# Logits through five banks in turn, and products with W in four 32-column tiles

## The chip, the cores and the metric

The kernel runs on one core of one Trainium2 chip. The metric is the time of one execution in device microseconds; the median of three runs before the change is 3207.64 us (3204.0 to 3208.25). The profile shows one further execution. Its engines are called PE (TensorE, the matrix array; PEld is its weight load), DVE (VectorE), ACT (ScalarE), POOL (GpSimd) and SP (SyncE, which issues most DMAs). PSUM, where TensorE writes its results, has eight banks of 128 partitions by 512 fp32 numbers; the kernel uses all eight.

## The reference

Sixteen graphs ("batches") of 1024 nodes with 256 features pass two layers. `adj` is 0 or 1. All arithmetic is fp32.

```python
x = _layernorm(x + L0_gnn(x, adj, ...))
x = _layernorm(x + L1_gnn(x, adj, ...))

# layer 0, 4 heads of 64
h = einsum('bnd,hde->bhne', x, W)
e_src = einsum('bhne,hte->bhtn', h, a_src); e_dst = einsum('bhne,hte->bhtn', h, a_dst)
weight = where(adj == 0, -1e9, leaky_relu(e_src[i] + e_dst[j], 0.01))
out = relu(softmax(weight) @ h + bias) + h
out = layer_norm_per_head(out) * ln_gamma + ln_beta

# layer 1, 8 heads of 32; queries, keys and values are the same normed rows
normed = layer_norm(x) * gamma1 + beta1
attn = softmax(where(adj > 0, q @ k.T / sqrt(32), -inf))
x = x + attn @ v
y = layer_norm(x) * gamma2 + beta2
out = x + gelu(y @ W1 + b1) @ W2 + b2          # 256 -> 1024 -> 256
```

## The kernel before

The kernel is one long program without loops on the chip. Two Python generators, `layer0` (line 1073) and `layer1` (1096), each yield after a small piece of work; a planner at the end of `fast_path` chooses whose piece comes next. Layer 0 works one batch ahead of layer 1, so that layer 0 of batch b+1 is laid between the pieces of layer 1 of batch b. The class `Pace` (92) keeps a running estimate of when each engine and each tile is free. It sets the order only: at run time each engine works through its own list in order, and waits where data or a buffer is not there yet. As all instructions are issued through one helper, the profile gives line 61 for all of them, and they are told apart by the names of their tiles.

Layer 0, per batch:

- `prepare` (528) takes the rows in four blocks of two times 128. Each block's x is transposed (`acc<-ident,xk`, copied to `xT` by ACT). For each of its two groups of 128 rows, two matmuls (halves c of the 256 features) multiply `xT` by `w0e` (W and the folded attention vectors, 264 columns) into one bank: `acc<-w0e,xT`, the "products with W". Between the two there is a yield, so the planner may put them into different gaps. ACT then takes four copies out of the bank (`apart`, `v`, `dinv`, `hb`), and DVE makes `z` and `v`. In the middle of each group `turn_mask` has ACT turn a loaded block of the adjacency into a byte mask (`mask<-ak`), and starts the load of the block three further on (a transposing DMA on SP's queue, three buffers). After each block the source terms are transposed (`acc<-ident,apart`) and pass through ACT (`rows`), memory (`esr`) and back (`cb`).
- `attention0` (646) has 32 steps, each of a pair of key blocks of one head. DVE makes the weights of a step (`p<-cb,dinv,mask`, two instructions), three steps ahead; TensorE multiplies them with `v` in 16 matmuls on 64-column tiles (`acc<-v,p`, 8 to a half step). A head's sums stay in one bank for its four steps, while the bank of the head before is read out.

Layer 1, per batch:

- `attention1` (804) has 32 steps. `exponentials` (822) computes four tiles of logits, 128 keys by 512 queries, as four concurrent matmuls on 32-row tiles (`ps<-nT`), and ACT takes each tile's exponential (`p<-ps`). One step later DVE multiplies with the mask (`p<-p,mask`, two a step). Three steps later (`LAG`) TensorE multiplies with the values on 32-column tiles: two heads with the exponentials moving (`po<-p,v` and `po<-p,unit`, four matmuls at once) and two with them held (`po<-v,p`, 32 matmuls of 33 columns). After every eighth step `heads_out` (904) copies the sums out (ACT `hs`, `oT`), transposes (`ident,oT`) and divides; `finish1` (931) normalises (ACT `o<-o,t,r`) and transposes.
- `mlp` (972) has matmuls on 64-column tiles, `ps<-yT,w_sb` with the GELU by ACT (`hid`), and `po<-w_sb,hid`.

The array of TensorE is thus used in four shapes: 32x128 (logits), 128x32 (attention 1's products), 64 columns (attention 0, MLP), and 128x128 (transposes, products with W).

PSUM is divided so: four banks `ps` in turn for the logits, the MLP's first stage and some transposes (ring `ps_s`); two banks `po`; and two single banks `acc0`, `acc1`, which `bank0` (395) hands out, the one taken longest ago first, unless it is `busy` with open sums. Layer 0 and, during attention 1, the transposes of layer 1 (`side_bank`, 408) use these two. Only in the last batch, when layer 0 has nothing left, do the logits take `acc0` and `acc1` too (`logits_tile`, 815).

The planner (1134 to 1178) counts progress: `WORK0` is layer 0's units per batch, `COURSE` says how far layer 0 should be at each point of layer 1, `SLACK` and `SLACK1` how far it may stray from that to fill a wait.

Of the kernel before, what the change touches and what calls it, by code (L numbers as in the profile page):

```python
# [31 lines left out]
F32 = mybir.dt.float32  # L32
# [7 lines left out]
P = 128  # L40
# [150 lines left out]
def fast_path(  # L191
# [24 lines left out]
    nc = Pace(tc.nc)  # L216
    B, N, D = x.shape
    H0, _, HO = w0.shape
# [176 lines left out]
    def bank0(shape, dtype=F32):  # L395
# [4 lines left out]
        return ps_a.tile(shape, dtype, f"acc{i}"), banks0[i]  # L400

    def bank0_ready():
        return min(ps_a.ready(f"acc{i}") for i in range(2) if not banks0[i]["busy"])
# [85 lines left out]
    def complete(chain):  # L489

        for item in list(chains):
            if item[0] is chain:
                while item in chains:
                    run(item)
# [33 lines left out]
    def prepare(b, hb, esr, cbs, v0, dinv, mask, first):  # L528
# [32 lines left out]
        for k in range(0, NB, GB):  # L561
# [13 lines left out]
            for g in range(GB):  # L575
# [6 lines left out]
                for c in range(DC):  # L582
                    nc.tensor.matmul(ph, xT[:, c, g * P : (g + 1) * P], w0e[:, c, :], start=c == 0, stop=c == DC - 1)
                    if c == 0:
                        if b:
                            turn_mask(k + g)
                        yield (0.45,)
                bank["busy"] = False
# [7 lines left out]
                if b == 0 and k == NB - GB:  # L596
                    first(g)
                yield 0.45, ready
                if g == 0 and b == 0:
# [204 lines left out]
    def attention1(half, values, mask, rinv, half_done, rest):  # L804
# [10 lines left out]
        def logits_tile():  # L815

            turn[0] = (turn[0] + 1) % 6
            if place[0][0] == B and turn[0] >= QUAD:
                return bank0([P, HALF])[0]
            return ps_s.tile([P, HALF], F32, name="ps")  # L820
# [46 lines left out]
        def logits_ready():  # L867
            return ps_s.ready("ps", QUAD)

        def outs_ready():  # L870
            return ps_o.ready("po", 2)

        for i in range(len(steps) + LAG):
            if i < len(steps):
                ready[i] = exponentials(*steps[i])
                advance()
# [256 lines left out]

    WORK0 = NB // GB * 2.0 + 2.0 + NB * H0 * 1.0
    REST1 = 3.5 * GB
    ATTN1 = REST1 + 2.0 + 2.5 * (NH * NB * H1 // QUAD)
    WORK1 = ATTN1 + NB // GB * (1.75 * FC / 2 + 3.5 * GB) - REST1
    SLACK = 0.083
    SLACK1 = 0.03
    STAY = 0.01  # L1140
    COURSE = [(0.0, 1.0), (REST1 + 1.0, 1.0), (ATTN1, 1.29), (WORK1 - 10.0, 2.0), (WORK1, 2.0)]

# [13 lines left out]
    while any(streams):  # L1156
# [5 lines left out]
        if all(streams):  # L1162
# [4 lines left out]
            if allowed and late[which] > max(late[other], 0.0) + 0.3:  # L1167
                which = other
        step = next(streams[which], None)
        if step is None:  # L1170
# [437 lines left out]
```

## Time and profile before

| | |
|---|---|
| median of three runs | 3207.64 us (3204.0 to 3208.25) |
| the profiled execution | 3203.7 us, span 3201.8 us |
| granted TensorE clock | 0.991 over the span |
| PE busy | 3148.4 us (98%), 67301 records |
| DVE busy | 2873.9 us (90%) |
| ACT busy | 1966.0 us (61%) |
| POOL busy | 497.8 us (16%) |
| DMA | 161.87 MB, 51 GB/s on the mean |

An fp32 matmul has two records here, since it is done in two passes with a weight load each; a transpose has one. A row of the timeline gives start, length, engine, line, operation, output <- inputs, the array's shape (rows*columns), the moving size and the count; what is in brackets is the engine's idle time before it and what ended it. A matmul's record is longer than the time between two starts, because matmuls are pipelined: intervals are read from start to start. Rows of windows give the stretch, its length, and then the busy time of PE, PEld, DVE, ACT and POOL, the granted clock, and the DMA's share and rate.

### The profile page before, as it was taken

What the parts mean: (1) busy time and instruction counts of PE and PEld (TensorE: products, weight loads), DVE (VectorE), ACT (ScalarE), POOL (GpSimd) and SP (SyncE); (2) the same over time, 40 slices, a digit from 0 to 9 for tenths busy, and PEclk for the clock granted to TensorE, in tenths of its full rate; (3) what the DMA queues carried; (4) which work ended last, traced back from release to release, by engine and by line L of the source; (5) the groups of instructions that cost most, each with busy time, mean ns of one, the idle gap of its engine ahead of it and who ended that gap; (6) DMA issues with size and microseconds to landing.
All of it is one profiled execution on the core that took longest, in us unless ns stands there. A gap on an engine that the chain in (4) does not pass through costs nothing.

```text
span 3201.8 us, 147006 instructions
## 1 busy us (share of the span) xinstructions
PE 3148.4 (98%) x67301; PEld 1966.1 (61%) x67301; DVE 2873.9 (90%) x4936; ACT 1966.0 (61%) x4258; POOL 497.8 (16%) x460
## 2 busy tenths in 40 slices
PE   6999999999999999999999999999999999999998
PEld 5557475565756657466575755757566575665745
DVE  6899998989989999899998989999899998999993
ACT  2664837648385673846748376483765838567383
POOL 1102011020211202112020110302112021120210
PEclk9799999999999999999999999999999999999999
DMA  7312203022130212203122031220302112010000
GB/s 156 78 26 65 53 26 88 20 68 49 32 85 23 71 40 58 65 20 77 31 71 53 26 85 23 68 50 26 91 17 75 43 46 75 20 48 20 28 10 16
DMA packets 208778, 161.87 MB, mean 51 GB/s; under 512 B 138322, under 2 KB 189522, under 8 KB 207188
## 3 DMA queue, kind: packets, MB, share of 16 engines
q1 hardware_dynamic: 200196, 115.66, 13.7%
q0 software_dynamic: 2592, 33.56, 5.3%
q8 instruction: 529, 8.67, 1.1%
q10 hardware_dynamic: 5360, 3.15, 0.4%
q14 instruction: 101, 0.83, 0.1%
HBM read 137.38 MB, written 48.50 MB: 58 GB/s over the span
## 4 chain that ended last, share of the span: by engine, by line
PE 96%; DVE 2%; issue 1%; DMA 1%; ACT 0%; POOL 0%; POOLq 0%; DVEq 0%; SPq 0%
PE po L61 39%; PE ps L61 33%; PE acc L61 24%; DVE p L61 1%; DVE hb L61 0%; DMA ak<-in_adj_dram 0%; DMA cb<-esr 0%; DMA esr<-rows 0%; ACT mask L61 0%; DVE relu L61 0%; DVE v0s L61 0%; DVE xl L61 0%; ACT sq L61 0%; ACT p L61 0%; ACT zz L61 0%
## 5 line engine op out<-in xcount | busy, mean ns | idle before, releaser
L61 DVE TENSOR_TENSOR p<-p,mask 128x1024 f32<-128x1024 f32 x1024 | 1186.3, 1217 | 1.3 <-ACT p L61 1.3
L61 ACT ACTIVATE p<-ps 128x512 f32<-128x512 f32 x2006 | 1041.9, 612 | 216.3 <-PE ps L61 201.3
L61 DVE SCALAR_TENSOR_TENSOR p<-cb,dinv,mask 128x512 f32<-128x512 f32 x1024 | 710.1, 744 | 8.6 <-DMA cb<-esr 8.4
L61 PE MATMUL ps<-nT 32*128 32x512 f32 x4012 | 627.4, 642 | 1.3 <-ACT p L61 1.3
L61 ACT ACTIVATE hid<-ps,b_sb 128x256 f32<-128x256 f32 x512 | 241.5, 472 | 610.9 <-PE ps L61 610.6
L61 PEld LDWEIGHTS acc<-v,p 128*64 128x64 f32 x16384 | 552.5, 140 | 77.8 <-DVE p L61 19.1
L61 PE MATMUL acc<-v,p 128*64 128x65 f32 x16384 | 575.6, 225 | 21.3 <-DVE p L61 16.8
L61 PEld LDWEIGHTS po<-v,p 128*32 128x32 f32 x32768 | 401.8, 109 | 316.5 <-issue 267.7
L61 PE MATMUL po<-p,v 128*32 128x512 f32 x2048 | 544.0, 606 | 0.0
L61 PE MATMUL po<-p,unit 128*32 128x512 f32 x2048 | 543.2, 606 | 0.0
L61 PE MATMUL ps<-yT,w_sb 128*64 128x256 f32 x4096 | 484.8, 380 | 0.0
L61 PE MATMUL po<-w_sb,hid 128*64 128x256 f32 x4096 | 481.4, 380 | 0.0
L61 PE MATMUL po<-v,p 128*32 128x33 f32 x32768 | 395.7, 198 | 8.5 <-issue 8.5
L61 POOL TENSOR_SCALAR r<-mv 128x4 f32<-128x4 f32 (+1 forms) x128 | 71.8, 561 | 2055.8 <-DVE mv L61 1852.4
L61 PEld LDWEIGHTS po<-w_sb,hid 128*64 128x64 f32 x4096 | 278.9, 137 | 141.9 <-issue 19.3
L61 PEld LDWEIGHTS ps<-yT,w_sb 128*64 128x64 f32 x4096 | 276.6, 137 | 124.5 <-issue 8.0
L61 POOL TENSOR_TENSOR r<-r,mhalf 128x8 f32<-128x8 f32 (+2 forms) x192 | 281.0, 1463 | 16.0
L61 PEld LDWEIGHTS po<-p,v 128*32 128x32 f32 x2048 | 78.2, 108 | 326.1 <-DVE p L61 153.2
L61 PEld LDWEIGHTS ps<-nT 32*128 32x128 f32 x4012 | 189.2, 183 | 128.7 <-ACT p L61 78.4
L61 PE MATMUL acc<-w0e,xT 128*128 128x264 f32 x480 | 167.0, 435 | 0.0
L61 POOL TENSOR_SCALAR r<-v0s 128x8 f32<-128x8 f32 x64 | 70.7, 1104 | 459.3 <-DVE v0s L61 458.1
L61 ACT ACTIVATE mask<-ak,shift_c 128x1024 uint8<-128x1024 bf16 x120 | 140.2, 1168 | 0.0
(121 smaller groups left out, 2454.3 us busy)
## 6 DMA issues: line engine op xcount, KB each, us to landing
cb<-esr SPq DMA_DIRECT2D x64, 512.0 KB
adjb<-in_adj_dram POOLq DMA_DIRECT2D x30, 1024.0 KB, 10.9
xk<-in_x_dram SPq DMA_DIRECT2D x64, 256.0 KB
xl<-in_x_dram SPq DMA_DIRECT2D x32, 512.0 KB
out_dram<-zz SPq DMA_DIRECT2D x64, 256.0 KB
ak<-adjb SPq DMA_TRANSPOSE x240
ak<-in_adj_dram POOLq DMA_DIRECT2D x8, 256.0 KB, 5.0
w_sb<-in_L_gnn_W_dram ACTq DMA_DIRECT2D x2, 1024.0 KB
```

The costliest lines, as they stand in the source:

```text
L61: return method(*args, **kwargs)
```

## The change

Three things change.

- The logits take five banks in turn: the four `ps` and a fifth. `lend` takes one of `acc0` and `acc1` from layer 0 when attention 1 of a batch begins, and `give_back` returns it after the last logits. While it is lent, layer 0 may go on to the point `PREP0` (the preparation and its first weights), and then the planner chooses layer 1 alone. The last batch, too, has five banks and not six.
- From the second batch on, a product with W is cut into four matmuls of 32 columns each. The yield between the two halves c is gone: a group of rows is one piece of eight matmuls.
- The planner's numbers follow: a group of rows counts 0.9 for its one piece, `WORK0` grows from 42 to 43, and `COURSE`, `SLACK` and `SLACK1` have other values.

```diff
@@ -399,6 +399,19 @@
         banks0[i].update(readers=[], taken=1 + max(bank["taken"] for bank in banks0))
         return ps_a.tile(shape, dtype, f"acc{i}"), banks0[i]
 
+    lent = []
+
+    def lend():
+        i = next(i for i in (1, 0) if not banks0[i]["busy"])
+        for chain in banks0[i]["readers"]:
+            complete(chain)
+        banks0[i].update(readers=[], busy=True)
+        lent.append(i)
+
+    def give_back():
+        i = lent.pop()
+        banks0[i].update(busy=False, taken=1 + max(bank["taken"] for bank in banks0))
+
     def bank0_ready():
         return min(ps_a.ready(f"acc{i}") for i in range(2) if not banks0[i]["busy"])
 
@@ -580,11 +593,17 @@
                 ph, bank = front_bank(b, [P, D + 2 * H0])
                 bank["busy"] = True
                 for c in range(DC):
-                    nc.tensor.matmul(ph, xT[:, c, g * P : (g + 1) * P], w0e[:, c, :], start=c == 0, stop=c == DC - 1)
-                    if c == 0:
-                        if b:
-                            turn_mask(k + g)
-                        yield (0.45,)
+                    for at in range(0, P, Q if b else P):
+                        m = Q if b else P
+                        nc.tensor.matmul(
+                            ph[at : at + m, :],
+                            xT[:, c, g * P + at : g * P + at + m],
+                            w0e[:, c, :],
+                            start=c == 0,
+                            stop=c == DC - 1,
+                        )
+                    if c == 0 and b:
+                        turn_mask(k + g)
                 bank["busy"] = False
                 nc.scalar.copy(apart[g][:, :, 0], ph[:, D + H0 : D + 2 * H0])
                 nc.scalar.activation(v0[:, k + g, :, HO], ph[:, D : D + H0], AF.Exp)
@@ -595,7 +614,7 @@
                 begin(scaling[-1], "vector", hb[-1])
                 if b == 0 and k == NB - GB:
                     first(g)
-                yield 0.45, ready
+                yield 0.9, ready
                 if g == 0 and b == 0:
                     turn_mask(k + 1)
                     yield 0.0, ready, xT
@@ -814,9 +833,9 @@
 
         def logits_tile():
 
-            turn[0] = (turn[0] + 1) % 6
-            if place[0][0] == B and turn[0] >= QUAD:
-                return bank0([P, HALF])[0]
+            turn[0] = (turn[0] + 1) % (QUAD + 1)
+            if turn[0] == QUAD:
+                return ps_a.tile([P, HALF], F32, f"acc{lent[0]}")
             return ps_s.tile([P, HALF], F32, name="ps")
 
         def exponentials(n, quad, jb):
@@ -865,12 +884,20 @@
         ready = {}
 
         def logits_ready():
-            return ps_s.ready("ps", QUAD)
+            free = [ps_s.ready("ps", i) for i in range(QUAD + 1)]
+            if not lent:
+                return free[QUAD]
+            wanted = [t % (QUAD + 1) for t in range(turn[0] + 1, turn[0] + 1 + QUAD)]
+            needs = ps_s.ready("ps", sum(t < QUAD for t in wanted))
+            return max(needs, ps_a.ready(f"acc{lent[0]}")) if QUAD in wanted else needs
 
         def outs_ready():
             return ps_o.ready("po", 2)
 
+        lend()
         for i in range(len(steps) + LAG):
+            if i == len(steps):
+                give_back()
             if i < len(steps):
                 ready[i] = exponentials(*steps[i])
                 advance()
@@ -1131,14 +1158,15 @@
 
 
 
-    WORK0 = NB // GB * 2.0 + 2.0 + NB * H0 * 1.0
+    WORK0 = NB // GB * 2.25 + 2.0 + NB * H0 * 1.0
+    PREP0 = NB // GB * 2.25 + 0.99
     REST1 = 3.5 * GB
     ATTN1 = REST1 + 2.0 + 2.5 * (NH * NB * H1 // QUAD)
     WORK1 = ATTN1 + NB // GB * (1.75 * FC / 2 + 3.5 * GB) - REST1
-    SLACK = 0.083
-    SLACK1 = 0.03
+    SLACK = 0.06
+    SLACK1 = 0.05
     STAY = 0.01
-    COURSE = [(0.0, 1.0), (REST1 + 1.0, 1.0), (ATTN1, 1.29), (WORK1 - 10.0, 2.0), (WORK1, 2.0)]
+    COURSE = [(0.0, 1.0), (REST1 + 0.0, 1.0), (ATTN1, 1.35), (WORK1 - 10.0, 2.0), (WORK1, 2.0)]
 
     def wanted():
         b, done = place[1]
@@ -1166,6 +1194,8 @@
             allowed = at0 < min(target + slack, place[1][0] + 2.05) if other == 0 else at0 > target - slack
             if allowed and late[which] > max(late[other], 0.0) + 0.3:
                 which = other
+            if lent and done0 >= PREP0:
+                which = 1
         step = next(streams[which], None)
         if step is None:
             streams[which], needs[which] = None, ()
```

## The prediction

> **What bounds the kernel now.** I read the page first: busy shares, then the chain that ended last.
>
> ```profile
> PE 3148.4 (98%) x67301; PEld 1966.1 (61%) x67301; DVE 2873.9 (90%) x4936; ACT 1966.0 (61%) x4258; POOL 497.8 (16%) x460
> ...
> PE 96%; DVE 2%; issue 1%; DMA 1%; ACT 0%; POOL 0%; POOLq 0%; DVEq 0%; SPq 0%
> ```
>
> TensorE is busy 98% and makes 96% of the chain, so only two things can move the end: the time TensorE needs for the same arithmetic, and the few waits it still has. The granted clock is full, so no clock term enters. Next, one batch split by stage (logits begin at 1087.5; the last two logits steps and the turn to the MLP lie in the second row; the MLP with layer 0's attention of the next batch in the third and fourth).
>
> ```profile
> 1087.00:1191.50 104.50, 104.50 (x2402) 53.29 (x2402) 93.72 (x141) 90.40 (x202) 9.73 (x10) 1.00 0.20 51
> 1191.50:1201.60 10.10, 10.10 (x353) 5.47 (x356) 10.10 (x11) 4.13 (x8) 0.00 (x0) 1.00 0.01 3
> 1201.60:1268.00 66.40, 66.40 (x1286) 52.60 (x1283) 63.23 (x132) 24.81 (x50) 18.64 (x17) 1.00 0.11 32
> 1268.00:1281.50 13.50, 13.50 (x188) 9.64 (x184) 12.09 (x27) 3.59 (x7) 3.15 (x3) 1.00 0.82 186
> ```
>
> The third number is PE, the fifth DVE, the sixth ACT. VectorE is close behind TensorE, and in the second row it has no idle time at all: the 98% hide a second bound. This batch takes 194.1 us (from its first logits at 1087.46 to the next batch's at 1281.59).
>
> Inside a stage I read TensorE's own timeline. Two stretches of attention 1, with and without a product with W (`w0e,xT`) between the products (`v,p`) and the next logits (`nT`):
>
> ```profile
> 1142.79 0.81 PE L61 MATMUL po<-v,p 128*32 128x33 f32 x64
> 1143.53 0.71 PE L61 MATMUL acc<-w0e,xT 128*128 128x264 f32 x2
> 1144.17 1.14 PE L61 MATMUL ps<-nT 32*128 32x512 f32 x8
> ...
> 1149.56 0.77 PE L61 MATMUL po<-v,p 128*32 128x33 f32 x64
> 1150.26 1.74 PE L61 MATMUL ps<-nT 32*128 32x512 f32 x8
> ```
>
> Start to start, products to logits takes 0.70 us without the W piece (1149.56 to 1150.26) and 1.38 with it (1142.79 to 1144.17): one piece costs 0.68. Its two passes of 264 columns need 0.22 each: the profile's passes of 512 columns start 0.45 apart (below), and 264/512 of that is 0.23. So about 0.2 us of every piece is the change of array shape, 128x32 to 128x128 to 32x128.
>
> The same stretch shows the only steady wait: logits take 1.14 undisturbed and 1.74 at 1150.26, because the fourth tile needs the last exponential of the step before. In this batch five logits steps are long (1.76, 1.74, 1.40, 1.65, 1.43): 2.3 us over 1.14 together. Adding up TensorE's start-to-start intervals over whole batches, I find some 190.5 us of pure work, 2.4 of such waits and 1 to 2 where products wait for a mask or weights from VectorE.
>
> **The change part by part.**
>
> *Products with W in column tiles.* By the two programs' orders of instructions, a batch has 16 single 128x128 products now: 13 stand alone between products and logits or transposes, three next to MLP work at the start. Afterwards there are 8 blocks of eight 32-column products; 6 stand directly behind the 128x32 products, without a change of shape, and 2 between logits and MLP. Their row is the nearest of the same shape:
>
> ```profile
> 1141.91 0.62 PE L61 MATMUL po<-p,v 128*32 128x512 f32 x1
> ...
> 1142.36 0.59 PE L61 MATMUL po<-p,v 128*32 128x512 f32 x1
> ```
>
> Four column tiles stream at once, and a pass of 512 takes 0.45. A block has four passes of 264: 4 x 0.225 = 0.90, plus some 0.02 at the change to logits that is there anyway: 0.92. Per batch, before: 13 x 0.65 (0.68 and, from the last product's start, 0.64) = 8.4, plus 1.6 for the other three; after: 6 x 0.92 + 2 x 1.0 = 7.5. Gain 2.5 us. Moves of other work nearly cancel: three of four transposes of source terms are parted from those of x (+0.15 each, a shape change more), and five half steps of layer 0's attention no longer stand between products and logits (-0.2 each); -0.4 to +0.5, taken as +0.1. Sum -2.4 a batch, 15 batches (the first batch's preparation keeps the full array): -36 us. It lies wholly on the path.
>
> A rule that speaks against it: the Trainium skill, "TensorEngine Tiling (Array Packing)", Performance Considerations, wants column tiles only where the stationary operand is at most 64 wide (here 128), and its Instruction Overhead puts about 60 cycles on each matmul. 720 more matmuls (960 for 240) at 60 cycles[...], 25 ns, would be 18 us as an estimate, so -18 instead of -36. The row of 64 records of 33 columns in 0.77 us (12 ns each at most, in four tiles) shows overheads of neighbouring tiles side by side, so I take -36 and keep -18 as an end.
>
> *The fifth bank.* Logits of a step then need only the third exponential of the step before, not the fourth. Exponentials follow each other 0.48 to 0.49 us apart (four in 2.06) and the first starts 1.16 after its logits (1147.61 to 1148.77). A bare step is 2.65 us (1147.61 to 1150.26). Fourth exponential: 1.16 + 2.06 + 0.05 = 3.27 after the logits' start, wanted at 2.67: the 0.60 above. Third: 2.78, so 0.11, and 0 in the step after one that waited. But bare steps become more: 84 of 512 logits follow products directly now, 237 after. I walked the 32 steps in ScalarE's new order with these intervals, a mask at 1.15, the four copies of a W block 0.4, head copies 0.75. W steps (2.65 + 0.92) hold exponentials, mask and copies (1.92 + 1.15 + 0.4 = 3.47) just within 3.57. What is left: the four `o` activations (2.08 in one row) now stand ahead of a bare step, 1.2 us; copies of heads 0.2; bare steps 0.7; and, with one bank fewer for everything else, the second W block of a batch waits about 0.45 for the copy of the first. Sum 2.7 against 2.4: +0.3. Ends: -1.2 (the long ones go too) and +2 (each late copy counts in full).
>
> *Layer 0 held back.* While a bank is lent, layer 0 stops at PREP0, so its attention runs wholly beside MLP. Queued behind VectorE there: 5 half steps' weights, 2.7 us of work, move from the first stage into the second; and TensorE has 56 MLP products instead of 40 behind the last step of layer 0, so weights must be done earlier.
>
> ```profile
> 1193.76 6.89 DVE L61 TENSOR_TENSOR p<-p,mask 128x1024 f32<-128x1024 f32 x6
> 1200.57 1.40 DVE L61 SCALAR_TENSOR_TENSOR p<-cb,dinv,mask 128x512 f32<-128x512 f32 x2
> 1202.72 0.20 DVE L61 RECIPROCAL ranges<-hs 128x8 f32<-128x8 f32 x1 [0.75 <-ACT hs L61]
> ```
>
> VectorE comes out of the masks about 6 us after the last logits begin; after the change I expect the same (6.3). The last weights are then 69.6 us of listed VectorE work later, 76 to 78.5 with 0 to 2.6 of its own idle time (now 2.5, of which the 0.75 above goes when VectorE arrives later); TensorE could use them at 75.6. Wait 0.4 to 3 us a batch, less 0.5 of now: I take +0.9.
>
> Course, slack and the new WORK0 cost no instruction; they only place the pieces, which is counted. DMAs are the same in number; masks' transposed loads stay three ahead, with two masks 3.5 us apart and then a pause, so nothing waits for them.
>
> Sum: -2.4 + 0.3 + 0.9 = -1.2 a batch, 15 batches -18; the last batch (five banks instead of six, no layer 0) 0 to +2. From the profiled execution's 3203.7 (span 3201.8, 1.9 around it) to 3186; the median of the runs lies 3.9 higher, 3207.6, and gives **3190**.
>
> **Rivals.**
> *Waits go with the bank.* If logits' waits fall to 1.2 and VectorE keeps up, only shapes and the bank count: -2.4 - 1.2 = -3.6 a batch, -54: 3154. For it: the fifth bank takes 0.5 of every long step. Against: three times as many bare steps.
>
> *VectorE becomes the bound (slower).* In the MLP stage, if it keeps its 2.5 us of idle and arrives 1.5 later, weights come 4.4 late instead of 0.5: +3.9 + 0.3 - 2.4 = +1.8 a batch, +27: 3235. It decides from 2.1 us more waiting than now. For it: 10.10 of 10.10 in the second row. Against: most of its idle is waiting for work that will be there.
>
> *One bank is too few for the side work (slower).* Some 23 W blocks and transposes a batch pass through it; from 0.1 us each the gain is gone, at 0.2 it is +2.2 a batch, +33: 3240. Against: most follow each other by a step of 2.65 and are copied out within 1 us.
>
> *The tiles gain half* (the rule above), with the same waits: -18 + 18: 3208, no change.
>
> **How the numbers follow.** The forecast 0.48, waits go 0.18, VectorE 0.15, one bank 0.07, half gain 0.12. About 0.2% (6.4 us) is what a measurement can tell from no change, 3201 to 3214. Range: from the first rival's 3154 to 3225, which leaves out the outer half of the slower cases. Faster: 0.18, nearly all of 0.48 and 0.03 of half gain: 0.67; same 0.12; slower 0.21. The likeliest case's own range is 3172 to 3204.
>
> **What would show it.** Right: a W group of 128x32 shape with passes 0.22 apart, held products to logits over a W block in 1.6 us; logits rows of 1.14 to 1.25 in most bare steps and one or two long ones beside the `o` activations; weights' waits (`acc` after `p`) up by about 1 us a batch; TensorE's batch near 193.2. Wrong: passes of W more than 0.3 apart, TensorE waiting for copies out of the single `acc` bank many times a batch, or gaps of several us before layer 0's products late in the MLP.

## The result, and the profile after

| | before | after |
|---|---|---|
| median of the runs shown with the result, us | 3207.9 (3204.0 to 3209.5) | 3170.3 (3166.4 to 3178.2) |
| profiled execution, its span, us | 3203.7, 3201.8 | 3170.4, 3168.6 |
| one batch, mean of the 2nd to the 15th, us | 194.9 | 192.8 |

The ratio is 0.9888 with a 95% interval of 0.9867 to 0.9909: the changed kernel is 1.1% faster. The sign was forecast rightly and the time lies in the range of 3154 to 3225 us, but the gain is 37.6 us where 17.6 were forecast, and the time lies just outside the likeliest case's own range (3172 to 3204). The size is what the experiments had to explain.

Two words are used below as in the prediction. A *W block* is the products with W of one group of 128 rows. A *bare step* is a step of layer 1's attention in which the logits follow the products directly, with no other work of TensorE between them.

The page of the changed kernel, its busy times and the shares of the chain that ended last:

```profile
PE 3114.9 (98%) x68741; PEld 1941.2 (61%) x68741; DVE 2877.3 (91%) x4936; ACT 1945.5 (61%) x4258; POOL 487.7 (15%) x460
...
PE 94%; ACT 3%; DVE 1%; DMA 1%; issue 1%; SPq 0%; POOL 0%; POOLq 0%; DVEq 0%
```

The list of groups, by shape, for the products with W, before and in tiles (after the bar busy us, mean ns of one, then idle time before them and what ended it):

```profile
L61 PE MATMUL acc<-w0e,xT 128*128 128x264 f32 x480 | 167.0, 435 | 0.0
...
L61 PE MATMUL acc<-w0e,xT 128*32 128x264 f32 x1920 | 132.1, 389 | 8.2 <-ACT hb L61 8.1 <-ACT rows L61 0.2
```

TensorE is still 98% busy, for 33.5 us less; VectorE is busy 3.4 us more and has the larger share. ScalarE, at 0% of the chain before, now makes 3% of it: the changed kernel has taken on waits for ScalarE. The W group shows one of them: it had no idle time ahead of it before, and now waits 8.1 us in all for `hb`, the last copy out of the one `acc` bank that is left.

One batch by stage, with the stretches of the prediction moved to this batch's first logits at 1074.6 and the last one ended at the next batch's (third number PE, fifth DVE, sixth ACT):

```profile
1074.15:1178.65 104.50, 104.02 (x2522) 51.15 (x2522) 94.65 (x144) 91.60 (x207) 10.14 (x9) 1.00 0.24 54
1178.65:1188.75 10.10, 9.88 (x381) 7.67 (x377) 10.10 (x13) 1.73 (x4) 0.00 (x0) 1.00 0.02 4
1188.75:1255.15 66.40, 66.40 (x1298) 52.67 (x1290) 65.54 (x138) 23.82 (x48) 15.53 (x15) 1.00 0.09 30
1255.15:1267.40 12.25, 12.25 (x117) 7.97 (x116) 9.51 (x18) 4.46 (x9) 4.58 (x5) 1.00 0.93 195
```

In the third row VectorE is busy 65.54 of 66.40 us, where it had 63.23 before. It has practically no idle time left from the end of layer 1's attention to the last weights of layer 0. The list of VectorE's waits in this part of the batch (us in all, times, longest) had three entries before the change and has none after it:

```profile
DVE hb L61 <- POOL r L61: 0.9, 1, 0.9
DVE ranges L61 <- ACT hs L61: 0.7, 1, 0.7
DVE zz L61 <- PE po L61: 0.7, 1, 0.7
```

The granted clock is still full, so the time is not a clock's.

TensorE's timeline over a W block shows the first step of the forecast as it was put: the products follow the W block's 16 records without a change of shape, and from products to logits it is 1.65 us (1109.04 to 1110.69; forecast 1.6).

```profile
1109.04 0.77 PE L61 MATMUL po<-v,p 128*32 128x33 f32 x64
1109.66 1.10 PE L61 MATMUL acc<-w0e,xT 128*32 128x264 f32 x16
1110.69 0.70 PE L61 MATMUL ps<-nT 32*128 32x512 f32 x3
```

The two waits that the forecast had named are there too, in the timeline of ScalarE and TensorE, at the second W block of the batch and beside the `o` activations:

```profile
1078.46 1.17 ACT L61 ACTIVATE mask<-ak,shift_c 128x1024 uint8<-128x1024 bf16 x1
...
1079.75 0.42 ACT L61 COPY hb<-acc 128x256 f32<-128x256 f32 x1
...
1080.23 1.10 PE L61 MATMUL acc<-w0e,xT 128*32 128x264 f32 x16 [0.48 <-ACT hb L61]
...
1153.11 2.08 ACT L61 ACTIVATE o<-o,t,r 128x256 f32<-128x256 f32 x4
...
1155.43 1.12 PE L61 MATMUL ps<-nT 32*128 32x512 f32 x3
...
1156.27 1.13 PE L61 MATMUL ps<-nT 32*128 32x512 f32 x2
```

The W block starts when the copy `hb` is done, which stands behind a mask of 1.17 us. The logits of 1155.43 need until 1157.76, when the transposes begin: 2.33 where undisturbed ones take 1.14, because four `o` activations of 2.08 us delayed the exponentials that free their banks.

VectorE's timeline at the end of layer 1's attention, where the forecast had it come late:

```profile
1175.91 8.03 DVE L61 TENSOR_TENSOR p<-p,mask 128x1024 f32<-128x1024 f32 x7
1183.86 5.38 DVE L61 SCALAR_TENSOR_TENSOR p<-cb,dinv,mask 128x512 f32<-128x512 f32 x8
...
1191.50 0.20 DVE L61 RECIPROCAL ranges<-hs 128x8 f32<-128x8 f32 x1
```

Masks end 6.8 us after the last logits begin (forecast 6.3). Then eight passes of layer 0's weights follow without a gap, and `ranges<-hs`, ahead of which VectorE stood idle for 0.75 us before the change, has no wait at all.

For the sum I took TensorE's start-to-start intervals over the 2nd to the 15th batch and set each against the median interval between the same two kinds of work in the profile before; what is over that is counted as waiting (the prediction's way, over 14 batches; rests under 0.1 are left out). In us per batch:

| | before | after | difference | forecast |
|---|---|---|---|---|
| work without waits, shape changes in it | 190.6 | 188.0 | -2.6 | -2.4 |
| logits waiting for a bank | 2.41 | 2.71 | +0.30 | with the next row +0.3 |
| W blocks waiting for their bank | 0 | 0.63 | +0.63 | |
| products waiting for masks | 1.02 | 0.44 | -0.58 | with the next row +0.9 |
| products of layer 0 waiting for weights | 0.70 | 0.87 | +0.17 | |
| all | 194.9 | 192.8 | -2.1 | -1.2 |

The last row is read directly from the timelines. How it is split over the rows above depends on the medians chosen, by up to some 0.5 us a row; sums of rows are firmer.

### The profile page after: what moved, and what is told of

Its sections match the earlier page's. It is cut to its first block, busy times and chain, and to the rows that moved or that the text cites. A ratio compares the mean times of both kernels' runs of the same rounds, so it can differ in the third digit from the quotient of the medians.

```text
span 3168.6 us, 150088 instructions
## 1 busy us (share of the span) xinstructions
PE 3114.9 (98%) x68741; PEld 1941.2 (61%) x68741; DVE 2877.3 (91%) x4936; ACT 1945.5 (61%) x4258; POOL 487.7 (15%) x460
## 4 chain that ended last, share of the span: by engine, by line
PE 94%; ACT 3%; DVE 1%; DMA 1%; issue 1%; SPq 0%; POOL 0%; POOLq 0%; DVEq 0%
PE po L61 39%; PE ps L61 29%; PE acc L61 26%; DVE p L61 1%; ACT p L61 1%; ACT mask L61 1%; ACT L61 1%; SPq L61 0%; DMA ak<-in_adj_dram 0%; DMA cb<-esr 0%; DMA adjb<-in_adj_dram 0%; DVE hb L61 0%; ACT hid L61 0%; POOL r L61 0%; ACT hb L61 0%
## 5 line engine op out<-in xcount | busy, mean ns | idle before, releaser
L61 ACT ACTIVATE p<-ps 128x512 f32<-128x512 f32 x1648 | 891.6, 617 | 152.9 <-PE ps L61 103.4
L61 PEld LDWEIGHTS acc<-v,p 128*64 128x64 f32 x16384 | 539.4, 140 | 70.8 <-DVE p L61 21.6
L61 PEld LDWEIGHTS po<-v,p 128*32 128x32 f32 x32768 | 393.6, 109 | 307.5 <-issue 264.7
L61 PE MATMUL acc<-v,p 128*64 128x65 f32 x16384 | 558.1, 225 | 23.4 <-DVE p L61 18.3
L61 PE MATMUL ps<-yT,w_sb 128*64 128x256 f32 x4096 | 477.9, 380 | 0.0
L61 PE MATMUL acc<-nT 32*128 32x512 f32 x800 | 449.1, 641 | 0.0
L61 POOL TENSOR_SCALAR r<-mv 128x4 f32<-128x4 f32 (+1 forms) x128 | 84.1, 657 | 2120.2 <-DVE mv L61 1861.6
L61 PE MATMUL po<-v,p 128*32 128x33 f32 x32768 | 385.9, 198 | 1.0 <-issue 1.0
L61 POOL TENSOR_TENSOR r<-r,mhalf 128x8 f32<-128x8 f32 (+2 forms) x192 | 302.0, 1573 | 16.0
L61 ACT ACTIVATE p<-acc 128x512 f32<-128x512 f32 x400 | 247.9, 620 | 45.8 <-PE ps L61 45.8
```

The source lines that it names most:

```text
L61: return method(*args, **kwargs)
```

## The experiments

All ratios are to the kernel before, run beside them; "a batch" is the mean of the 2nd to the 15th in the profiled run.

### Taking the change apart

**Full-array passes again (e2).** The changed kernel with

```diff
-                    for at in range(0, P, Q if b else P):
-                        m = Q if b else P
+                    for at in range(0, P, P):
+                        m = P
```

> The changed kernel with its W products as two full-array 128x128 passes again, in one piece; bank, hold and the order of everything else as in the changed kernel (237 bare steps). Theory (the tiles' gain is the change of shape of some 0.2 us at each of the standalone products, 120 x 0.17 = 20 us in the sum of TensorE's work): 3188 to 3192, and the profile shows products to logits over one piece in about 1.7 us against 1.6. Rival (four times as many matmuls cost their own overhead, so tiles are worth half or nothing): 3170 to 3180.

Measured 3184.0 us, 0.9937 (0.9924 to 0.9951); 13.7 us more than the changed kernel. Its timeline, TensorE over one block: from products to logits it is 1.76 us (1107.98 to 1109.74).

```profile
1107.98 0.75 PE L61 MATMUL po<-v,p 128*32 128x33 f32 x64
1108.66 1.16 PE L61 MATMUL acc<-w0e,xT 128*128 128x264 f32 x4
1109.74 0.70 PE L61 MATMUL ps<-nT 32*128 32x512 f32 x2
```

The two kernels have the same order of work, so their intervals can be set side by side: the W blocks cost 1.1 us a batch more with the full array, 16 us in all, of the theory's 20, and the whole batch is 0.9 us longer. The median lies between the two ranges: the tiles are worth some 14 us, over a third of the gain. The overhead of more matmuls is not seen; the rest of the gain does not need the tiles.

**Tiles and one piece alone (e1), full-array one piece alone (e3).** The kernel before with the edit below; e3 has `range(0, P, P)` and `m = P` in it.

```diff
-                    nc.tensor.matmul(ph, xT[:, c, g * P : (g + 1) * P], w0e[:, c, :], start=c == 0, stop=c == DC - 1)
-                    if c == 0:
-                        if b:
-                            turn_mask(k + g)
-                        yield (0.45,)
+                    for at in range(0, P, Q if b else P):
+                        m = Q if b else P
+                        nc.tensor.matmul(ph[at : at + m, :], ...)
+                    if c == 0 and b:
+                        turn_mask(k + g)
...
-                yield 0.45, ready
+                yield 0.9, ready
```

> The first part of the change alone: products with W in 32-column tiles and one piece, on the kernel before, with its four logits banks and layer 0 running on beside attention 1. Pure work of TensorE falls by 43 us by the shapes that are no longer changed, but the steps in which logits follow the products directly rise from 84 to 189, and with four banks each one behind a filled step waits about 0.6 us. Theory (the shapes pay only together with the fifth bank): most of the gain is eaten, 3180 to 3205 us, with logits rows of 1.7 us and over in most bare steps. Rival (the bank is worth little; the shapes alone make the gain): 3160 to 3170, as the whole change or better.

> The kernel before with its two half pieces of a W block joined to one, full-array passes, four banks, no hold. Joining saves 23 us of shape changes in TensorE's work and makes 189 bare steps of 84. Theory (with four banks a bare step costs about 0.6 us of waiting, which is more than a joined piece saves): no faster than before, 3205 to 3225. Rival (waiting is small): 3182 to 3190.

Measured 3355.6 (1.0466, 1.0452 to 1.0480) and 3381.2 (1.0548, 1.0534 to 1.0563). The sign is the theory's, the size is far beyond it. A batch of e1 is 10.8 us longer: logits wait 8.5 us instead of 2.4, which is the bank, and products of layer 0 wait 6.9 instead of 0.7, which nobody had forecast. The list of waits of e1 (us in all, times, longest) names the second:

```profile
PE acc L61 <- DVE relu L61: 82.0, 16, 5.3
```

and its timeline, VectorE and TensorE, shows it:

```profile
1457.29 1.22 DVE L61 TENSOR_TENSOR o<-o,x 128x1024 f32<-128x1024 f32 x1
1457.39 0.64 PE L61 MATMUL acc<-v,p 128*64 128x65 f32 x16
1458.55 1.41 DVE L61 BATCH_NORM_STATS2 st<-o 128x6 f32<-128x256 f32 x4
...
1462.80 0.42 DVE L61 SCALAR_TENSOR_TENSOR relu<-acc,ranges 128x256 f32<-128x256 f32 x1
...
1463.37 2.00 PE L61 MATMUL acc<-v,p 128*64 128x65 f32 x32 [5.34 <-DVE relu L61]
```

Joining the pieces made the kernel's planner place the first head of layer 0 so that the next one needs the same `acc` bank at once. The instruction that frees it, `relu`, is queued on VectorE behind the statistics of layer 1's output. TensorE waits 5.3 us for it, once a batch.

The clock adds to that. With each such wait TensorE's granted clock falls to half for 3.4 to 6.8 us, in each of the 14 batches from the 2nd to the 15th, while it stays full from the second batch on in the kernels before and after the change. The stretch behind the wait shown above (the clock is the third number from the end):

```profile
1463.40:1468.00 4.60, 4.60 (x45) 3.52 (x46) 3.09 (x6) 2.56 (x5) 0.00 (x0) 0.50 0.35 113
```

Outside the waits 4.2 us a batch run at half clock, so that some 2.1 us are lost (an estimate: half of them), in part inside the 6.9. e3 has the same waits and the same drops. So e1 measures the change's first part together with an order that the change avoids, not the first part alone.

**The bank taken back (e4).** The changed kernel with

```diff
-            turn[0] = (turn[0] + 1) % (QUAD + 1)
-            if turn[0] == QUAD:
-                return ps_a.tile([P, HALF], F32, f"acc{lent[0]}")
...
-        lend()
+        lent.append(0)
...
-                give_back()
+                lent.pop()
```

and `logits_ready` as before the change. `lent` now only holds layer 0 back.

> The changed kernel without the fifth bank: logits on four banks, both acc banks for the side work, layer 0 still held back for the length of layer 1, tiles as in the changed kernel. 297 bare steps. Theory (the bank takes about 0.5 us of waiting from each bare step): logits waits rise from 2.7 us to 6 to 8 us a batch, 3220 to 3250 us. Rival (layer 0's hold or VectorE, not the bank, is what counts): 3165 to 3185.

Measured 3240.8, 1.0112 (1.0096 to 1.0127): inside the theory's range. Logits wait 8.0 us a batch against 2.7. In its timeline a bare step behind a filled one is long:

```profile
1132.77 1.09 PE L61 MATMUL acc<-w0e,xT 128*32 128x264 f32 x15
1133.79 1.14 PE L61 MATMUL ps<-nT 32*128 32x512 f32 x8
1135.74 0.75 PE L61 MATMUL po<-v,p 128*32 128x33 f32 x64
1136.42 1.77 PE L61 MATMUL ps<-nT 32*128 32x512 f32 x8
```

The logits at 1136.42 take 1.77 (forecast for a bare step with four banks: 1.14 + 0.60). So the change without its bank is 70 us slower, twice the whole gain: tiles in one piece make bare steps, and bare steps need the bank. The order is not quite the same, since the planner counts with the banks: e4 has 297 bare steps and the changed kernel 237. The 70 us are the bank and these steps together.

**The hold alone (e11), and four banks without it (e10).** e11 is the kernel before with

```diff
+            if lent and done0 >= PREP0:
+                which = 1
```

where `lent` is filled at the start of layer 1's attention and emptied behind its last logits, and `PREP0 = NB // GB * 2.0 + 0.99`. e10 is e1 with the changed kernel's `WORK0`, `SLACK`, `SLACK1` and `COURSE`.

> The kernel before with layer 0 held back for the length of layer 1's attention and nothing else of the change: half pieces, four banks, the course of before. It shows the third step of the sum alone. Work of TensorE 3053.4 us (7 less), 174 bare steps of 84, which with four banks cost some 3 us a batch more. Theory A (as forecast: the work that moves to the second stage makes VectorE late, 0.9 us a batch more waiting for its weights and masks than before): waits for weights and masks of 2.5 to 3 us a batch, 3255 to 3265. Theory B (VectorE only gives up idle time; waits of products for masks and weights together do not grow): 1.0 to 1.6 us a batch, 3235 to 3250.

> The kernel before with products in tiles and one piece and with the changed kernel's numbers for course and slack, four logits banks, layer 0 not held. It differs from the kernel with four banks and layer 0 held by the hold alone (and the order that follows), and from the kernel with the first part alone by the course. Its work of TensorE is 3029.8 us, 159 bare steps. Theory (the 6.7 us a batch that products of layer 0 waited for weights in the kernel with the first part alone come from where the course puts the first products of layer 0 behind the last masks, not from the tiles): those waits fall to 0.3 to 1.5 us a batch, logits waits are 5 to 7, 3220 to 3240 us. Rival (without the hold VectorE comes late in any case): waits for weights of 4 us and more a batch, 3270 to 3330.

e11 measured 3229.3, 1.0070 (1.0053 to 1.0087), below both ranges and nearer to theory B. A batch is 1.6 us longer: work -0.5, logits +2.0. Waits for weights go from 0.70 to 1.41 and those for masks from 1.02 to 0.52: together +0.2 (with other medians -0.2) where the forecast had +0.9. This is the step on which theory A and the prediction stood. It costs next to nothing, because what the weights lose the masks get back.

e10 measured 3253.8, 1.0153 (1.0136 to 1.0170). Waits for weights are under 1 us a batch, so e1's 6.9 came from the course and slack, as its theory said. Its range was missed by 14 us because `relu` collides elsewhere: transposes wait 2.3 us a batch for it, and in 7 of the 14 batches the clock falls to half behind that wait (another 0.9 us a batch, estimated as for e1). e4 is 13 us faster than e10, but that is not the price of the hold alone, since e10 has this collision and 159 bare steps where e4 has 297.

### Is VectorE at its limit?

**Six passes added beside the MLP, to the changed kernel (e5) and to the kernel before (e15).**

```diff
+            if b and i in (12, 18):
+                for _ in range(3):
+                    nc.nc.vector.tensor_mul(spare, spare, spare)
```

in layer 0's attention, `spare` being 128x256 fp32.

> The changed kernel with six more VectorE passes over 128x256 elements of a spare tile in each batch from the second on (about 0.33 us each, 2.0 us together), three at each of two steps of layer 0's attention, where it runs beside the MLP; the order of all other work is the same. Theory A (VectorE has lost its idle time in this stage and sets when the last weights come, so every further us there is a us of TensorE's waiting): 1.5 to 2.0 us a batch, 3192 to 3200 us, and products waiting for weights (acc after p) up by as much. Theory B (VectorE is far enough from the bound that it takes 2 us without loss, so the waits forecast for it could not come): 3168 to 3176.

> The kernel before with the six VectorE passes over a spare tile beside the MLP in each batch that cost the changed kernel 29 us (2.5 us a batch by their measured 0.42 us each). Theory A (before the change VectorE's 2.5 to 4.5 us of idle time in that stage was real slack, which the hold then used up): part of the passes goes into the idle time, 0 to 1 us a batch, 3207 to 3222 us. Theory B (its idle time there was waiting for work that came late, so VectorE set the last weights before the change as well): 1.7 us a batch and more, 3230 to 3245 us.

One pass took 0.424 us, so 2.5 us a batch and 38 us in all. e5 measured 3199.7, 0.9976 (0.9966 to 0.9986): 29 us more than the changed kernel, 77% of what was added, and in theory A's range. e15 measured 3226.5, 1.0063 (1.0049 to 1.0077): 21 us, 56%, between A and B. The list of waits shows where it went, in the weight loads of layer 0's products (us in all, times, longest). The changed kernel:

```profile
PEld acc L61 <- DVE p L61: 21.6, 21, 3.5
```

and with the passes, e5:

```profile
PEld acc L61 <- DVE p L61: 33.5, 70, 3.0
```

The kernel before, and with the passes, e15:

```profile
PEld acc L61 <- DVE p L61: 19.1, 15, 3.3
...
PEld acc L61 <- DVE p L61: 41.5, 60, 2.9
```

By the intervals, waits for weights rise from 0.87 to 2.64 us a batch in e5, and little else moves. So VectorE sets the last weights after the change, and in part it did so before. Of the 2.5 us a batch, 1.1 disappeared in slack before the change and 0.6 after it: the change used up about half of the slack that was there, and ran over it by little.

**The same passes in layer 1's attention (e6)**, at `if i in (5, 10)` there.

> The same six VectorE passes over a spare tile (2.0 us a batch), but at two steps early in layer 1's attention, where VectorE has some 9 us of idle time a batch. Both theories: no change, 3168 to 3175 us; more would show that VectorE's whole time, not its place, counts.

Measured 3202.4, 0.9986 (0.9979 to 0.9993): 32 us, as much as beside the MLP (here for 41 us of passes, as the first batch has them too). Both theories missed. Waits for masks cost 0.4 to 0.5 us more a batch, and 1.6 us appear at one place, in front of a transpose at the thirteenth step. VectorE's and TensorE's timeline shows what it waits for:

```profile
1127.31 0.42 DVE L61 TENSOR_TENSOR o<-acc,ranges 128x256 f32<-128x256 f32 x1
...
1127.88 0.41 PE L61 MATMUL acc<-ident,apart 128*128 128x128 f32 x2 [1.46 <-DVE o L61]
```

It is the bank. `o<-acc,ranges` reads the heads' sums out of the one `acc` bank that is left, and behind the added passes VectorE comes to it late. So the 9 us of VectorE's idle time in that stage are not room for more work at this place: what VectorE does there frees a bank that TensorE wants next. This much of e6 is the single bank's doing; whether the same passes cost as much with two `acc` banks was not tested.

**One VectorE addition given to GpSimd (e12).**

```diff
+        args = x1, x1, b2_r[:, None, :].to_broadcast([P, BPH, D])
+        if n:
+            nc.vector.tensor_add(*args)
+        else:
+            nc.nc.gpsimd.tensor_add(*args)
+            yield "vector", at_time(nc.now() + 30.0)
+            nc.enter("vector", "tensor_add", args, {})
```

> The changed kernel with one of VectorE's 128x1024 additions of each batch (x and the second bias, first half, 1.13 us, now in the stage beside the MLP) done by GpSimd early in that stretch; TensorE's and ScalarE's orders are the same. It takes work away from the stage to which the run with added passes brought some. Theory (VectorE sets the last weights there): products' waits for weights fall from 0.86 us a batch towards their floor of 0.26, 0.4 to 0.6 us a batch, 3161 to 3165 us. Rival 1 (the waiting that is left comes from the order, not from VectorE's amount of work): 3168 to 3172. Rival 2 (the addition on GpSimd holds VectorE up): above 3173.

Measured 3202.8, 0.9990 (0.9984 to 0.9997): rival 2. The addition also begins earlier: 76 us after the batch's first logits, still in layer 1's attention. In its timeline GpSimd's pass takes 2.50 us, and VectorE stands still beside it:

```profile
1161.36 2.50 POOL L981 TENSOR_TENSOR x<-x,b_r 128x1024 f32<-128x1024 f32 x1
1161.54 2.33 DVE L61 SCALAR_TENSOR_TENSOR t<-mv,r 128x4 f32<-128x4 f32 x1
...
1164.59 2.35 DVE L61 TENSOR_TENSOR p<-p,mask 128x1024 f32<-128x1024 f32 x2
...
1165.86 0.62 PE L61 MATMUL po<-p,v 128*32 128x512 f32 x1 [0.83 <-DVE p L61]
```

`t<-mv,r` over 128x4 elements, 0.15 us in the changed kernel, takes 2.33 and ends 0.02 us after GpSimd's pass, in all sixteen batches. The masks behind it come late and TensorE waits, some 3 us a batch more for masks; logits wait 1.4 us less, and a batch is 1.9 us longer. So the edit took 1.1 us a batch from VectorE beside the MLP and put 2.2 upon it in layer 1's attention (its busy time is 2895.4 us, 18.1 more), where, as in e6, TensorE soon feels it. What the same 1.1 us less beside the MLP are worth stays untested.

### The two waits that the change adds

**Mask behind the copies (e8), and also the `o` activations parted (e9), and also the addition on GpSimd (e13).**

```diff
-                    if c == 0 and b:
-                        turn_mask(k + g)
...
                 nc.scalar.copy(h, ph[:, 0:D])
+                if b:
+                    turn_mask(k + g)
```

e9 has besides a `yield "scalar", at_time(...)` between the four activations of `finish1`, and its second pair of transposes may come 2 us later.

> The changed kernel with ScalarE's mask of a W block issued after the four copies out of the block's bank, not before them; nothing else is edited, the order shifts a little with it (279 bare steps, 237 before). Theory (the second W block of a batch waits for the copies of the first out of the one acc bank, and the mask of 1.15 us ahead of them is that wait): the wait of 0.63 us a batch falls to 0.1 or less, 3158 to 3165 us. Rival (the late mask meets the exponentials of the next logits): logits waits grow by as much, 3168 to 3176.

> As the last, and the four activations over `o` (2.1 us in one row on ScalarE, ahead of a bare step, where the logits row of 1.2 us extra is) parted, one to a step. Theory: that row goes back to 1.2 us or less, another 0.6 to 1.1 us a batch, 3145 to 3156 us. Rival (the two pairs of transposes behind them now wait for the one acc bank and give it back): as the last run within 4 us.

> As the last, with the addition on GpSimd too. Theory (three separate waits, so the gains add): below the last run by as much as the addition alone gained, 3138 to 3152 us. Rival (TensorE is then early everywhere and VectorE's stage takes the gains back): as the last run within 3 us.

Measured 3278.5 (1.0224, 1.0210 to 1.0238), 3300.8 (1.0286, 1.0272 to 1.0300) and 3336.7 (1.0410, 1.0396 to 1.0424): no theory's number was near. (The addition on GpSimd costs e13 36 us over e9, about what it cost e12.) In each the planner, which prices ScalarE's new order, laid the transposes differently; e8's timeline shows the price:

```profile
1116.00 0.66 PE L61 MATMUL acc<-ident,sq 128*128 128x128 f32 x4 [0.32 <-ACT nT L61]
...
1118.60 1.18 ACT L61 ACTIVATE nT<-acc,be_c,g_c 128x256 f32<-128x256 f32 x2
1119.83 1.11 PE L61 MATMUL acc<-ident,xk 128*128 128x128 f32 x4 [3.17 <-ACT nT L61]
```

Two groups of transposes stand in a row on the one `acc` bank, and the copy between them waits on ScalarE behind four exponentials. TensorE stands still for 3.2 us, and with this wait, too, the clock falls to half for 3.4 to 6.8 us, in each of the 14 batches of e8, e9 and e13. That is some 2.3 of the 7.7 us by which a batch of e8 is longer than the changed kernel's (estimated as for e1). This is the prediction's rival "one bank is too few for the side work", real in this order and absent in the changed kernel's, where a step lies between such groups. These three runs say nothing about the two waits.

**The same edits with the order held (e14, e16, e17, e18).** The planner is told of the work in the old place (`nc.enter(...)`), and the instruction is issued in the new one, so the orders of TensorE, VectorE and GpSimd are the changed kernel's and only ScalarE's differs. `issue` is called behind the copies, and what is left in `deferred` behind the next four exponentials:

```diff
+            nc.enter("scalar", "activation", args, more)
+            if later:
+                return issue
...
+            deferred.append(lambda args=args, more=more: nc.nc.scalar.activation(*args, **more))
+            if not lent or g < GB:
+                flush()
```

e14 has the masks alone, e16 both, e17 `o` alone, e18 `o` and the mask of a batch's first W block alone. The changed kernel ran beside the last two.

> The changed kernel with ScalarE's mask of a W block behind the four copies out of the block's bank, as in the earlier run, but with the planner's books unchanged, so that TensorE, VectorE and GpSimd have exactly the changed kernel's order and only ScalarE's is edited. Theory (the 0.63 us a batch at the second W block is the mask in front of the copies; the earlier run lost its time by the other order of transposes that the planner chose): the wait falls below 0.15, -0.5 us a batch, 3160 to 3166 us. Rival (the mask behind the copies makes exponentials late): 3168 to 3176.

> As the last edit of the changed kernel (mask behind the copies), and the third and fourth of the four activations over `o` behind the exponentials of the step, the first two before them, again with TensorE's, VectorE's and GpSimd's orders untouched. Theory (the four in one row delay the exponentials by their 2.08 us and make the one long logits step of a batch, 1.2 us): half of the delay goes, 0.5 to 0.9 us a batch below the last edit alone, 3148 to 3158 us. Rival (the other two delay the next step's exponentials instead): as the mask's edit alone within 3 us.

> The changed kernel with only the third and fourth `o` activations behind the exponentials of the step (masks as in the changed kernel); no other engine's order is touched. Theory (the gain of 8.8 us that this edit brought on top of the mask's holds here too): the 1.26 us at the long logits step falls below 0.3, masks and weights take back some tenths, 3159 to 3165 us. Rival (VectorE, with no idle time left, takes it all back): 3168 to 3172.

> As the last, and the mask of the batch's first W block alone behind that block's copies: the one that the second block waits for. Theory (only there does the mask stand before a wait; behind the copies of the other blocks it only delayed exponentials): another 0.2 to 0.5 us a batch below the last kernel, 3152 to 3161 us. Rival (VectorE's weights come late by as much): as the last within 2 us.

> The changed kernel itself, beside the two edits of it on the same chip: 3166 to 3175 us.

| kernel | median, us | ratio to before (95%) |
|---|---|---|
| e14, all masks | 3176.0 | 0.9906 (0.9891 to 0.9921) |
| e16, all masks and `o` | 3167.3 | 0.9883 (0.9867 to 0.9898) |
| changed kernel beside e17, e18 | 3169.3 | 0.9887 (0.9872 to 0.9902) |
| e17, `o` alone | 3162.6 | 0.9867 (0.9852 to 0.9882) |
| e18, `o` and the first mask | 3157.9 | 0.9851 (0.9838 to 0.9864) |

e14 is its rival: the wait at the W block goes (0.63 to 0.1), but logits wait 3.7 us a batch instead of 2.7. (Its interval overlaps the changed kernel's; the mean batch is 0.3 us longer.) In its timeline the mask behind the copies holds up the exponentials that free the logits' banks, and the logits at 1131.88 take 1.83:

```profile
1129.81 1.18 ACT L563 ACTIVATE mask<-ak,shift_c 128x1024 uint8<-128x1024 bf16 x1
...
1130.95 1.59 ACT L61 ACTIVATE p<-ps 128x512 f32<-128x512 f32 x3
1131.88 1.83 PE L61 MATMUL ps<-nT 32*128 32x512 f32 x8
```

e16 lies 8.8 us below e14, as its theory had the step, though from a higher base. e17 is its theory, within the range: the long logits step is gone. ScalarE's timeline of e18, which has the same edit, shows the activations in two pairs with the exponentials between them:

```profile
1148.38 1.10 ACT L984 ACTIVATE o<-o,t,r 128x256 f32<-128x256 f32 x2
1149.36 0.61 ACT L61 ACTIVATE p<-ps 128x512 f32<-128x512 f32 x1
...
1151.27 1.14 ACT L984 ACTIVATE o<-o,t,r 128x256 f32<-128x256 f32 x2
```

Logits wait 1.6 us a batch instead of 2.7, but a batch is only 0.5 shorter: waits for masks take back 0.4 and those for weights 0.2. Argued, not shown apart: VectorE has no time left, so that an earlier TensorE runs into it. e18 beats both kernels, 11.4 us below the changed one on the same chip, with no run of the one in the range of the other. Its wait at the W block is 0.1, but the transposes behind it wait 0.4 more, so the mean batch of its profile is that of e17. Of the further 4.7 us between the medians the two profiled executions show 2.3, nearly all of it in the first batch and its start; why there was not tested. So e18's time lies in its theory's range, but not for the theory's reason.

## Why the prediction was right or wrong

**The products in column tiles: right.** Forecast -2.4 us a batch, measured -2.6. The row that it was read from, 128x32 passes, held; the estimate of 18 us from the overhead of each matmul did not show. e2 puts the array shape's part at 1.1 us a batch. The rest of the 2.6, from joining the two pieces of a block and from moves of other work, was not measured alone.

**The fifth bank: the mechanism right, the size short.** Logits wait 2.7 us a batch, with one step of 1.2 beside the `o` activations, as put. But in that 2.7 the wait at the second W block had been included; it comes on top, at 0.63 where 0.45 was forecast. So the step is +0.9, not +0.3 (0.30 + 0.63). e4 shows what hangs on the bank: 5.3 us a batch of waiting for logits, in an order with 60 more bare steps.

**Layer 0 held back: this step failed.** "Wait 0.4 to 3 us a batch, less 0.5 of now: I take +0.9." Measured: weights +0.17, masks -0.58, together -0.4. The last weights come 76.2 us after the last logits, at the low end of "76 to 78.5", because VectorE's own idle time, put at "0 to 2.6", fell to almost nothing: the forecast took a middle of a range whose end was the likely case. Its idle gaps had been waits for the heads' sums (`hs`), for GpSimd's `r` and for the MLP's sums (`zz<-po`), the three lines above; arriving later, VectorE finds all of them ready. And the step counted only what VectorE does later. That VectorE has fewer of layer 0's weights between the last masks, so that products wait less for masks, was left out. Before the change about half of the waits for masks, 0.5 us a batch, stood at the last logits step, where weights lay between the last masks; after it next to nothing is left there, and with the hold alone (e11) 0.1. e11 as a whole shows the exchange (weights +0.7, masks -0.5). The difference to the forecast, 1.3 us in 14 batches, is 18 us.

**The ends.** The first batch became 5.4 us shorter (202.6 to 197.2), where the sum had given it the common 1.2; the last 0.6 longer, within 0 to 2. The first batch's waits before were some 18 us, and the sum did not look at them; after the change they are some 11. Why they fell was not tested.

**From the profiled execution to the median.** 3.9 us were added because the median before lay that far above its profiled run; after the change the two agree within 0.1. That is the chance of which execution was profiled, and no mechanism.

Together, against the forecast of 3190: the hold -18, the fifth bank with the W block +9, tiles and shapes -3, the first batch -4, the offset -4, the start and the last batch +1: -19 of the 19.7 missed, the rest rounding. Some 8 of these (first batch and offset) have nothing to do with the argument of the prediction, and two errors of the argument, the hold and the bank, partly cancel.

**The rivals.** "Waits go with the bank" did not happen: waits rose by 0.5 a batch; that the result lies half way to its 3154 has the other reasons above. "VectorE becomes the bound" is true as a state and false as a price: e5 shows that what is added to VectorE is paid at 77%, but the change added only what its slack took. "One bank too few" cost 0.63 us a batch and can cost several in orders close by (3.2 us at one place in e8), or when VectorE is late (1.6 in e6). "Half gain" by the price of each matmul fell with e2: with a quarter of the matmuls the kernel is slower, not faster.

## What to carry to other kernels

When work moves to an engine that is nearly full, count its idle gaps by what ends them: gaps that wait for late work vanish when the engine arrives later, before the engine delays anyone. Look at both sides of the queue, at what comes later and at what it no longer stands in front of. And where a planner lays the order, an experiment must hold that order, by telling the planner of the old place and issuing in the new one; otherwise it measures the planner: the same edit gave 3278 us with the order free and 3176 with it held.

## What the runs showed of the hardware

A GpSimd pass over 128x1024 fp32 elements in SBUF (2.50 us) stopped VectorE for its whole length in sixteen of sixteen places, though VectorE's own work there was 128x4 elements. The Trainium skill, "SBUF — State Buffer", section "SBUF: two separate sides", describes an exclusive lock on the port pair that the two share, held for the whole instruction; it names VectorE operations with two inputs from SBUF as ones that need the pair against a GpSimd operation that reads SBUF; `t<-mv,r` has two such inputs, and the addition on GpSimd reads x and the bias. The run agrees, with 2.33 us for an operation of 0.15. So moving work from a full VectorE to an idle GpSimd made VectorE fuller, by 18 us.

Sixteen 32-column records of 264 columns, four tiles at once, take 1.03 us from their start to the next logits' (1109.66 to 1110.69), against 1.08 for four full-array records (1108.66 to 1109.74): four times as many matmuls of a quarter of the width show no overhead of their own.

A long wait of TensorE cost more than its own length. With waits of 5.3 us (e1, e3) and 3.2 us (e8, e9, e13) the granted clock was half for 3.4 to 6.8 us in every one of 14 batches, at the end of the wait and beyond it; with waits of 2.3 us (e10) it was half for 3.4 us in 7 of 14; with waits of up to 1.6 us (e6) never. What decides it between 1.6 and 3.2 us, these runs do not show.
